# Layer 0 of a two-layer graph network with experts: which queue loads the fixed places, and when the last list writes are issued

## The chip, the cores and the metric

The kernel runs on one core of a Trainium2 chip. The metric is the device time of one execution in microseconds (us), as the median of several runs. Before the change it is 1020.93 us, the median of three runs of 1011.31, 1020.93 and 1027.31 us. A separate execution was taken by the profiler: 1022.18 us, of which 1020.1 us lie between its first and its last instruction (the span). All times in the trace count from the start of that span.

## What is computed

There are 3327 nodes with 256 features each, and a 0/1 adjacency matrix. Two layers follow each other, each with a graph step and a step of routed experts, and each adds its result to its input:

```python
# --- layer 0 (adj_ffn) ---
x = x + _L0_gnn_ref(_layernorm(x, axis=-1), adj, L0_gnn_W, L0_gnn_b)
x = x + _L0_ffn_ref((_layernorm(x, axis=-1))[None], L0_ffn_gate_w, L0_ffn_gate_b, L0_ffn_w1, L0_ffn_w2, L0_ffn_w3)[0]
# --- layer 1 (adj_ffn) ---
x = x + _L1_gnn_ref(_layernorm(x, axis=-1), adj, L1_gnn_W, L1_gnn_a)
...
# _L0_gnn_ref
a = (adj == 1).astype(x.dtype)
deg = jnp.sum(a, axis=1, keepdims=True)
agg = jnp.einsum('ij,jf->if', a, x) / deg
return agg @ W.T + b
...
# _L0_ffn_ref: 16 experts, 256 -> 512 -> 256
probs = jax.nn.softmax(logits, axis=-1)
top_probs, top_idx = jax.lax.top_k(probs, 2)
top_probs = top_probs / jnp.sum(top_probs, axis=-1, keepdims=True)
dispatch = jnp.sum(jax.nn.one_hot(top_idx, n_experts, dtype=x.dtype) * top_probs[..., None], axis=-2)
h1 = jnp.einsum('bsd,edh->bseh', x, w1)
h2 = jnp.einsum('bsd,edh->bseh', x, w2)
hidden = jax.nn.silu(h1) * h2
expert_out = jnp.einsum('bseh,eho->bseo', hidden, w3)
return jnp.einsum('bseo,bse->bso', expert_out, dispatch)
```

The change touches the experts of layer 0 alone.

## The kernel before

Nodes are handled in 26 tiles of 128, taken in chunks of four tiles (the last chunk has two). The graph step of layer 0 (`graph`, line 746) runs over three blocks of chunks: the first three chunks, the fourth, and the last three. For each block it streams the transposed adjacency matrix from memory through SP's queue (`load_adj`, three buffers), DVE turns each piece into a mask (line 698), and TensorE multiplies it with the normalised nodes (line 815). When a block is complete, its chunks go through small closing steps: divide, project, normalise, store the rows in `hd`, compute the gate's logits and route (`dispatch`).

Routing writes a list per expert into `list0` in memory. Each entry is three numbers: where the node's result goes, which row of `hd` to read, and the node's weight. `dispatch` computes each entry's position, and `listed` (line 364) writes 128 entries in one indirect transfer on POOL's queue (line 366). A tile needs two of these, one per chosen expert. For the last block (ten tiles, 20 list writes) the writes are not issued at once: they are put in the list `due` and dealt out later.

The experts of layer 0 then run in slots of up to 256 entries of one expert (`slots0`, line 1095). The first ten slots are fixed: the first 256 entries of experts 0 to 9, all of which come from tiles of the first two blocks. So they start before the last block has been routed. Their entries, the places, are loaded together into the tile `whos` by `routed0` (line 969), which is called before group 21 of the last block's 26 adjacency groups: two transfers on ACT's queue, one for experts 0 and 1 and one for experts 2 to 9. Both depend on the list writes of the first two blocks. Slots from 10 on are chosen by a table and their places are loaded by `places0` on SP's queue; these read lists that must be complete, so they wait for the last list write.

What a slot does, and on which engine:

- `rows_in0` (line 1019): two indirect gathers on POOL's queue bring the slot's rows from `hd` into `xg` (three buffers). They need the slot's places.
- `turned0` (line 1029): TensorE turns the rows (line 1036), half a slot per gather, and ACT copies the result.
- `hidden0` (line 1041), twice, one half of the hidden features each: TensorE (line 1048), then ACT and DVE. The experts' weights come through SP's queue, three transfers of 512 KB per expert (line 998).
- `out0` (line 1066): TensorE (line 1071), DVE scales by the weight (line 1076), and two indirect transfers on POOL's queue add the rows to `xd` in memory (line 1078).

`slots0` yields after each half slot. In the round of slot s it issues the gathers of slot s + 2, turns the rows of slot s + 1, computes the first half of slot s (first yield), closes slot s - 1 with its two adds, and computes the second half of slot s (second yield). `beside` (line 1197) drives it for the first eight slots while the closing steps of the last block are dealt out between, three per half slot. There it also deals out the list writes in `due`. The counter i starts at 1 with the first half of slot 0, so i = 5 and 6 are the halves of slot 2. The deal is three writes per half slot from i = 9 on, the first half of slot 4.

POOL's queue works strictly in the order in which the program issues, and on it lie the list writes, the gathers and the adds. Semaphores that mark transfers as landed are shared in turn: eight for the transfers of SP and ACT together, eight for POOL's. A transfer is issued only when the one that last used its semaphore has landed.

Of the kernel before, what the change touches and what calls it, by code (L numbers as in the profile page):

```python
# [19 lines left out]
P = 128  # L20
# [5 lines left out]
def kernel(  # L26
# [26 lines left out]
    nc = tc.nc  # L53
    N, D = x.shape
    E0, _, H0 = ffn0_w1.shape
    E1, _, H1 = ffn1_w1.shape
# [3 lines left out]
    NP = NT * P  # L60
# [13 lines left out]
    def last_rows():  # L74
# [24 lines left out]
    SA = 2 * P  # L99
    AHEAD_E = 5 * E0 // 8  # L100
# [20 lines left out]
    lists = [  # L121
        dram.tile([E * NP + 2 * P, 3], I32, name=f"list{i}") for i, E in enumerate((E0, E1))
    ]
# [118 lines left out]
    last = {}  # L242
    due = []
# [150 lines left out]
    def rank_table(seen):  # L394

        ps = ps_mm.tile([P, 512], F32, name="mm")
        nc.tensor.matmul(ps[:, :E0], ones_h, seen, start=True, stop=True)

        def small(name, w=E0, dtype=F32):
            return work.tile([P, w], dtype, name=name, bufs=1)  # L400

        key, rank, rest, junk, at = small("k_key"), small("k_rank"), small("k_rest"), small("k_junk"), small("k_at", 2)
        nc.vector.scalar_tensor_tensor(key, ps[:, :E0], float(E0), order_e, op0=OP.mult, op1=OP.add)
        more_ = io.tile([P, 2, D], F32, name="y", bufs=2)[:, 0, : E0 * E0].rearrange("p (a b) -> p a b", b=E0)
        nc.vector.tensor_tensor(more_, key[:, None, :].to_broadcast([P, E0, E0]), key[:, :, None].to_broadcast([P, E0, E0]), op=OP.is_gt)
        nc.vector.tensor_reduce(rank, more_, AX.X, OP.add)
        for i, values in enumerate((rev[:, 0, :], start_e[:, 0, :])):
            nc.vector.scalar_tensor_tensor(junk, rank, slot_p[:, 0:1], values, op0=OP.is_equal, op1=OP.mult, accum_out=at[:, i : i + 1])
        out = small("k_out", 3, I32)
        nc.vector.tensor_scalar(out[:, 0:1], at[:, 0:1], -1.0, float(E0), op0=OP.mult, op1=OP.add)  # L410
        nc.vector.tensor_copy(out[:, 1:2], at[:, 1:2])
        nc.vector.tensor_scalar(out[:, 2:3], at[:, 1:2], float(SA), None, op0=OP.add)
        nc.vector.tensor_scalar(rest, ps[:, :E0], -float(SA), None, op0=OP.add)
        return out, rank, rest
# [132 lines left out]
    def asked(table, s, col=3, name="more"):  # L547

        with in_order(), ExitStack() as behind:
            for name in ("slot", "dve", "act", "pool"):  # L550
                behind.enter_context(tc.issue_after(last[name].ins))
            _, (is_one,) = nc.values_load_multi_w_load_instructions(table[s : s + 1, col : col + 1], min_val=0, max_val=1, bass_reorder=False)
            tc.mark_branch_hint_location(f"{name}{s}", "LikelyTaken", [e.engine for e in (nc.tensor, nc.vector, nc.scalar, nc.gpsimd, nc.sync)])
        return is_one, f"{name}{s}"
# [9 lines left out]
    def in_turn_on_pool():  # L564

        return tc.issue_after(last["pool"].ins) if "pool" in last else nullcontext()
# [383 lines left out]
    early = {}  # L950
# [8 lines left out]
    def places0(s):  # L959

        _, table, row, col, _ = plan[s]
        who = io.tile([P, 2, 3], I32, name="who", bufs=8)
        with in_order():
            at = nc.sync.value_load(early[table][row : row + 1, col : col + 1], min_val=0, max_val=E0 * NP)
        with in_order():
            last["who"] = nc.sync.dma_start(who, lists[0][bass.ds(at, SA), :].rearrange("(h p) w -> p h w", p=P))
        return who

    def routed0():

        with tc.issue_after(last["adj"].ins):
            load0_hidden(0)
        whos = io.tile([P, AHEAD_E, 2, 3], I32, name="whos", bufs=1)
        of = lists[0][: E0 * NP, :].rearrange("(e n) w -> e n w", n=NP)[:, :SA, :].rearrange("e (p h) w -> p e (h w)", p=P)
        for lo, hi in ((0, 2), (2, AHEAD_E)):
            nc.scalar.dma_start(whos[:, lo:hi].rearrange("p e h w -> p e (h w)"), of[:, lo:hi])
        for s in range(AHEAD_E):
            who[s] = whos[:, s]

# [11 lines left out]
    def starts(s):  # L991
        return plan[s][0] != plan[s - 1][0] if s else True

    def next_run(s):
        return next((i for i in range(s + 1, len(plan)) if starts(i)), len(plan))
# [4 lines left out]
    def load0_hidden(s):  # L1000
        run, table, row, _, _ = plan[s]
        if table is None:
            which[run] = slice(run, run + 1)
        else:
            with in_order():
                which[run] = bass.ds(nc.sync.value_load(early[table][row : row + 1, 0:1], min_val=0, max_val=E0 - 1), 1)
        with in_order():
            for i, w in enumerate((ffn0_w1, ffn0_w2)):
                load0(s, i, w[which[run]].rearrange("o (p k) h -> p (o k) h", k=KD))

    def load0_out(s):
        with in_order():
            load0(s, 2, ffn0_w3[which.pop(plan[s][0])].rearrange("o (a p b) d -> p (o a) b d", p=P, b=2))
# [5 lines left out]
    def rows_in0(s):  # L1019
        xg = io.tile([P, 2, D], F32, name="xg", bufs=3)  # L1020
        for h, m in parts0(s):
            with in_turn_on_pool():
                last["pool"] = nc.gpsimd.indirect_dma_start(  # L1023
                    out=xg[:m, h, :], out_offset=None, in_=hd_of[0][: NE0 * P, :] if s < AHEAD_E else hd[:, :],
                    in_offset=bass.IndirectOffsetOnAxis(ap=who[s][:m, h, 1:2], axis=0),
                )
        return xg
# [67 lines left out]
    def slots0(first, end):  # L1095
        usual = not first
        for s in range(first - 3, end + 1):
            if usual and s in AHEAD_AT:
                graph1_ahead(AHEAD_AT.index(s))
            if usual and s == AHEAD_E - 2:  # L1100
                early["rank"], *early["ranks"] = rank_table(seen0)
            if usual and s == AHEAD_E + 2:
                early["spill"] = spill_table(*early["ranks"], seen_head)
            if usual and s == end - 2:
                early["more"] = asked(early["spill"], 0)
            if s == first - 1 and first:
                load0_hidden(first)
            if first <= s < end and starts(s):
                if next_run(s) < end:
                    load0_hidden(next_run(s))  # L1110
                load0_out(s)
            known = AHEAD_E if s < AHEAD_E - 2 else end
            for i in range(max(who, default=-1) + 1, min(s + 4, known)):
                who[i] = places0(i)
            for i in range(max(xg, default=-1) + 1, min(s + 3, known)):
                xg[i] = rows_in0(i)
            if first <= s + 1 < end:
                xT[s + 1] = turned0(s + 1, xg[s + 1])
            if first <= s < end:
                hid[s] = [hidden0(s, xT[s], 0)]  # L1120
                if usual:
                    head1(2 * (s - LATE0))
                yield
            if first <= s - 1:
                out0(s - 1, hid.pop(s - 1))
            if first <= s < end:
                hid[s].append(hidden0(s, xT.pop(s), 1))
                if usual and s == end - 1:
                    spare = const.tile([P, 1], F32, name="spare")
                    nc.scalar.activation(spare, half[:, 0:1], AF.Exp, bias=hid[s][1][:, 0, 0:1], scale=0.0)  # L1130
                if usual:
                    head1(2 * (s - LATE0) + 1)
                yield
            elif s == first - 1:
                yield


# [49 lines left out]
    def graph1_ahead(i):  # L1187
        with in_order():
            a = load_adj(pools1[1], GRAPH[0], groups_of(GRAPH[0])[i])
        if i < AHEAD:  # L1190
            ahead1[1][0, i] = mask_of(a, pools1[2], GRAPH[0], groups_of(GRAPH[0])[i], 0.0, OP.not_equal)
        else:
            ahead1[0][0, i] = a

    slots = slots0(0, USUAL0)

    def beside(post):

        for i, _ in enumerate(slots, 1):
            for _ in range(3):  # L1200
                next(post, None)
            for _ in range(3 if i > 8 else 0):
                if due:
                    due.pop(0)()
            if i == 2 * (AHEAD_E - 2):
                break
        assert not due and next(post, None) is None
# [200 lines left out]
```

## Time and profile before

| What | Value |
|---|---|
| Median of three runs | 1020.93 us (1011.31 to 1027.31) |
| Profiled execution | 1022.18 us |
| Its span | 1020.1 us |
| Mean granted TensorE clock | 0.961 |
| Busy time of DVE, ACT, POOL | 493.1, 257.6, 429.7 us |
| Issue of the two places' transfers on ACT | 200.2 and 200.7 us |
| First gather of slot 0 | 202.94 us |
| First and last list write of the last block | 277.93 and 322.29 us |
| Mean of one list write on POOL (line 366) | 1057 ns, 104 of them |
| Median of one gather of the fixed slots (line 1023) | 977 ns, 20 of them |
| Mean of one add of the fixed slots (line 1078) | 1619 ns, 20 of them |

How to read it: an engine's busy time counts its instructions alone; a wait is put down to the event that came last before the instruction could start. The time of a transfer on POOL's queue in the timeline is the time in which POOL builds it; the data land later, and that is given as the time from issue to landing. In lines of the timeline the columns are start, length, engine, line of the kernel, operation, what is written and read, how many were merged, and in brackets the idle time before and what ended it. Tables of stretches give, for each stretch, its length, the busy time of PE, PEld (weight load of TensorE), DVE, ACT and POOL, the granted clock, the DMA engines' busy share and GB/s.

### The profile page before, as it was taken

Reading aid. Unit: us, or ns where it says so; the run is one execution under the profiler, and the core shown is the slowest. Engines: PE = TensorE matmul, PEld = TensorE weight load, DVE = VectorE, ACT = ScalarE, POOL = GpSimd, SP = SyncE. Lnnn points to the kernel's source line nnn. Section 1 sums busy time; section 2 is a strip of 40 time slices with the busy share of each in tenths; the row PEclk is TensorE's granted clock in tenths of the full one; section 3 lists DMA queues with packets and bytes.
Section 4 is the critical chain, followed back from the end, with each engine's and each line's share of the span. In section 5 each row is a group of like instructions: output and inputs, shape, how many; then the busy total and the mean of one; then the engine's idle time right before and its main releaser. Section 6 shows DMA issues by size and latency. Waiting matters only on the chain. (4 is left out here: it accounts for less than half of the span.)

```text
span 1020.1 us, 14285 instructions
## 1 busy us (share of the span) xinstructions
PE 931.9 (91%) x4505; PEld 783.9 (77%) x4505; DVE 493.1 (48%) x1797; ACT 257.6 (25%) x530; POOL 429.7 (42%) x407
## 2 busy tenths in 40 slices
PE   7899999899997999999999999999889578999991
PEld 5677887688886999888987777877667357888880
DVE  7565585254622322212123577667576541343764
ACT  3310311024311111111111444130222323444440
POOL 2040062522476454454453311005251475777762
PEclk9999999898998999999999999999899789999996
DMA  9988677856677656677888398868954865333376
GB/s 335 326 299 285 230 181 234 236 176 200 183 160 165 192 161 149 162 207 211 225 262 251 76 312 285 254 211 188 253 110 150 256 180 166 95 94 93 93 260 209
DMA packets 109328, 207.00 MB, mean 203 GB/s; under 512 B 30595, under 2 KB 63044, under 8 KB 109246
## 3 DMA queue, kind: packets, MB, share of 16 engines
q1 hardware_dynamic: 68384, 157.30, 49.3%
q0 software_dynamic: 20528, 30.56, 13.3%
q10 hardware_dynamic: 20334, 18.17, 6.1%
q8 instruction: 36, 0.59, 0.3%
q14 instruction: 46, 0.38, 0.2%
HBM read 176.82 MB, written 35.47 MB: 208 GB/s over the span
## 5 line engine op out<-in xcount | busy, mean ns | idle before, releaser
L815 PE MATMUL acc<-big,y 128*128 128x512 f32 (+2 forms) x1456 | 344.9, 391 | 25.4 <-DVE big L698 15.0
L815 PEld LDWEIGHTS acc<-big,y 128*128 128x128 f32 (+1 forms) x1456 | 265.0, 194 | 82.0 <-ACT y L871 9.0
L1048 PE MATMUL acc<-xT,w 128*128 128x256 f32 (+3 forms) x1024 | 213.3, 362 | 0.0
L1048 PEld LDWEIGHTS acc<-xT,w 128*128 128x128 f32 x1024 | 186.0, 200 | 16.5 <-issue 3.5
L366 POOL DMA_INDIRECT list<-where,t_idx x104 | 109.9, 1057 | 187.3 <-DVE t_idx L361 63.1
L698 DVE TENSOR_SCALAR big<-adj 128x1536 fp32r<-128x1536 int32 (+6 forms) x130 | 111.7, 864 | 118.0 <-DMA adj<-in_adj_t 79.9
L1071 PE MATMUL acc<-w,hid 128*128 128x256 f32 (+3 forms) x512 | 118.0, 381 | 0.0
L1056 DVE TENSOR_TENSOR hid<-hid,acc 128x512 f32<-128x512 f32 (+3 forms) x64 | 40.0, 624 | 145.3 <-PE acc L1048 138.3
L1078 POOL DMA_INDIRECT xd<-y,who x44 | 67.7, 1539 | 100.0 <-DVE y L1076 64.0
L1071 PEld LDWEIGHTS acc<-w,hid 128*128 128x128 f32 (+3 forms) x512 | 89.1, 178 | 20.1 <-issue 3.6
L1052 ACT ACTIVATE hid<-acc 128x512 f32<-128x512 f32 (+3 forms) x64 | 35.0, 547 | 212.7 <-PE acc L1048 200.1
L620 POOL DMA_INDIRECT zd<-y,who x58 | 70.6, 1218 | 29.2 <-DVE y L1291 16.1
L1277 ACT ACTIVATE h<-acc,v 128x256 f32<-128x256 f32 x116 | 54.9, 474 | 102.8 <-PE acc L1274 101.8
L1274 PE MATMUL acc<-xT,v 128*128 128x256 f32 x232 | 63.6, 398 | 6.1 <-DMA v<-w1d 5.5
L595 POOL DMA_INDIRECT xg<-hd,who x58 | 57.2, 986 | 26.4 <-issue 21.3
L1274 PE MATMUL acc<-h,v 128*128 128x256 f32 x232 | 61.1, 387 | 0.6 <-ACT h L1277 0.6
L1289 DVE TENSOR_TENSOR y<-acc,v 128x512 f32<-128x512 f32 x29 | 20.0, 691 | 81.5 <-PE acc L1286 81.5
L270 POOL TENSOR_TENSOR ln_var<-ln_var,half 128x2 f32<-128x2 f32 (+2 forms) x19 | 15.2, 802 | 102.5 <-DVE ln_var L268 80.6
L1078 POOL DMA_INDIRECT xd<-y,whos x20 | 32.4, 1619 | 60.5 <-DVE y L1076 42.5
L1286 PE MATMUL acc<-v,h 128*128 128x256 f32 x232 | 56.7, 387 | 0.1
L1274 PEld LDWEIGHTS acc<-xT,v 128*128 128x128 f32 x232 | 44.6, 203 | 14.8 <-issue 5.3
L1023 POOL DMA_INDIRECT xg<-hd,who x44 | 43.0, 977 | 18.8 <-issue 11.0
(282 smaller groups left out, 970.7 us busy)
## 6 DMA issues: line engine op xcount, KB each, us to landing
adj<-in_adj_t SPq DMA_DIRECT2D x66, 768.0 KB, 6.3
w<-in_ffn_w SPq DMA_DIRECT2D x78, 512.0 KB, 5.8
adj<-in_adj_t SPq DMA_DIRECT2D x25, 639.5 KB, 6.7
adj<-in_adj_t SPq DMA_DIRECT2D x25, 512.0 KB, 4.6
v<-w1d SPq DMA_DIRECT2D x7, 898.0 KB, 9.3
hd<-ln_h ACTq DMA_DIRECT2D x12, 512.0 KB, 10.7
w_all<-w1d SPq DMA_DIRECT2D x6, 898.0 KB, 15.6
w1d<-in_ffn_w ACTq DMA_DIRECT2D x18, 256.0 KB, 5.3
```

Of the source, the lines that this page charges most:

```text
L366: ins = nc.gpsimd.indirect_dma_start(out=rows_of[2 * (t0 + j) + i], out_offset=bass.IndirectOffsetOnAxis(ap=idx[:, i, j : j + 1], axis=0), ...
L595: last["pool"] = nc.gpsimd.indirect_dma_start(out=xg[:, h, :], out_offset=None, in_=of, in_offset=bass.IndirectOffsetOnAxis(ap=who[:, h, 1 ...
L620: last["z"] = nc.gpsimd.indirect_dma_start(out=zviews[n * s + h], out_offset=bass.IndirectOffsetOnAxis(ap=who[:, h, 0:1], axis=0), in_=y[: ...
L698: last["mask"] = nc.vector.tensor_scalar(mask[:kr, :, :cols], a[:kr, :, :cols], value, None, op0=op)
L815: last["graph"] = nc.tensor.matmul(acc[c][k][:, :w], y[:kr, j, part, k * P : (k + 1) * P], mask[:kr, jj, i0 : i0 + w], start=(j == 0 and p ...
L1023: last["pool"] = nc.gpsimd.indirect_dma_start(out=xg[:m, h, :], out_offset=None, in_=hd_of[0][: NE0 * P, :] if s < AHEAD_E else hd[:, :], ...
L1048: last["slot"] = nc.tensor.matmul(q[:, c, :n], w[:, k, h0 : h0 + 2 * P - 1 : 2], xT[:, k, :n], start=(k == 0), stop=(k == KD - 1))
L1071: nc.tensor.matmul(ps[:m, h, :], hid[c // 2][:, c % 2, h * P : h * P + m], w3[:, c // 2, c % 2, :], start=(c == 0), stop=(c == NC0 - 1))
L1078: ins = last["pool"] = nc.gpsimd.indirect_dma_start(out=xd_of[2 + h] if s < USUAL0 else xd, out_offset=bass.IndirectOffsetOnAxis(ap=who[s] ...
L1274: ins = nc.tensor.matmul(ps[:, c, :], w[:, k, c : H1 : NC1], src[:, k, :], start=(k == 0), stop=(k == 1))
L1277: last["act"] = nc.scalar.activation(dst[:, c, :], ps[:, c, :], AF.Relu, bias=w1s[s % 3][:, BB + 2 * i + c : BB + 2 * i + c + 1])
L1286: nc.tensor.matmul(ps[:, h, :], h2[:, c, h * P : (h + 1) * P], w[:, c, :], start=(c == 0), stop=(c == NC1 - 1))
```

## The change

The places of the fixed slots are loaded on POOL's queue instead of ACT's. The first transfer (experts 0 and 1) stands where both stood before; the second (experts 2 to 9) is issued from `slots0` at s = -1, behind the gathers of slots 0 and 1. Both are kept in turn with POOL's other indirect work.

The 20 list writes of the last block are dealt from i = 6 on, the second half of slot 2: 5, 3, 4, 3, 3 and 2 at i = 6 to 11.

```diff
+    def fixed_places(lo, hi):
+
+        of = lists[0][: E0 * NP, :].rearrange("(e n) w -> e n w", n=NP)[:, :SA, :].rearrange("e (p h) w -> p e (h w)", p=P)
+        with in_turn_on_pool():
+            last["pool"] = nc.gpsimd.dma_start(early["whos"][:, lo:hi].rearrange("p e h w -> p e (h w)"), of[:, lo:hi])
+
     def routed0():
 
         with tc.issue_after(last["adj"].ins):
             load0_hidden(0)
         whos = io.tile([P, AHEAD_E, 2, 3], I32, name="whos", bufs=1)
-        of = lists[0][: E0 * NP, :].rearrange("(e n) w -> e n w", n=NP)[:, :SA, :].rearrange("e (p h) w -> p e (h w)", p=P)
-        for lo, hi in ((0, 2), (2, AHEAD_E)):
-            nc.scalar.dma_start(whos[:, lo:hi].rearrange("p e h w -> p e (h w)"), of[:, lo:hi])
+        early["whos"] = whos
+        fixed_places(0, 2)
         for s in range(AHEAD_E):
             who[s] = whos[:, s]
...
             elif s == first - 1:
+                if usual:
+                    fixed_places(2, AHEAD_E)
                 yield
...
+    DEALT = {6: 5, 7: 3, 8: 4, 9: 3, 10: 3, 11: 2}
+
     def beside(post):
 
         for i, _ in enumerate(slots, 1):
             for _ in range(3):
                 next(post, None)
-            for _ in range(3 if i > 8 else 0):
-                if due:
-                    due.pop(0)()
+            for _ in range(DEALT.get(i, 0)):
+                due.pop(0)()
             if i == 2 * (AHEAD_E - 2):
                 break
```

## The prediction

> **What bounds the kernel now.** I read the page first, then the waits of TensorE in the stretch that the diff touches, then that stretch on TensorE and on POOL in order of time, and last SP's queue.
>
> ```profile
> PE 931.9 (91%) x4505; PEld 783.9 (77%) x4505; DVE 493.1 (48%) x1797; ACT 257.6 (25%) x530; POOL 429.7 (42%) x407
> ```
>
> TensorE is busy 91% of the 1020.1 us span; a change that adds no matmul can win only at its gaps. The diff acts between about 200 us (the places are loaded) and 323 us (the last list write). TensorE's waits from 196 to 345 us (total, times, longest):
>
> ```profile
> PE acc L1036 <- DMA xg<-hd,whos: 7.4, 3, 4.5
> PE acc L815 <- DVE big L700: 4.4, 1, 4.4
> PE mm L1036 <- DMA xg<-hd,whos: 1.1, 1, 1.1
> ```
>
> L1036 turns a slot's gathered rows. So 8.5 us go to gathers that land late. The 4.4 us (194 to 198 us) end with a mask whose adjacency load was issued at 184.37 us, before anything changed; it stays. TensorE in order of time (start, length, idle before):
>
> ```profile
> 297.87 0.51 PE L1036 MATMUL acc<-ident,xg 128*128 128x128 f32 x2 [1.64 <-DMA xg<-hd,whos]
> ...
> 319.41 0.17 PE L397 MATMUL mm<-seen,ones_h 128*128 128x16 bf16 x1
> 324.13 0.67 PE L1036 MATMUL acc<-ident,xg 128*128 128x128 f32 x2 [4.54 <-DMA xg<-hd,whos]
> 326.06 0.70 PE L1036 MATMUL acc<-ident,xg 128*128 128x128 f32 x2 [1.25 <-DMA xg<-hd,whos]
> 326.55 5.31 PE L1048 MATMUL acc<-xT,w 128*128 128x256 f32 x16
> ```
>
> Slot 7 (slots counted from 0) costs 12.74 us from hidden layer to hidden layer (285.47 to 298.21) where the undisturbed step is 10.83 (298.21 to 309.04): 1.91 lost. Slot 9 starts at 326.55 where 309.04 + 10.83 = 319.87 would do: 6.68 lost. Its first 16 matmuls take 5.31 us instead of 3.63, another 1.68: the granted clock was 0.50 from 324 to 328 us. Together **10.27 us**, all that the new dealing can win. After 327 us TensorE has no gap until 552 us, so what is won or lost here moves the rest of the layer.
>
> POOL in the same stretch shows why the gathers are late:
>
> ```profile
> 260.34 1.57 POOL L1078 DMA_INDIRECT xd<-y,whos  x1 [0.30 <-DVE rden L761]
> 262.21 1.00 POOL L1023 DMA_INDIRECT xg<-hd,whos  x1 [0.30 <-issue]
> 263.52 0.97 POOL L1023 DMA_INDIRECT xg<-hd,whos  x1 [0.30 <-issue]
> 271.53 1.62 POOL L1078 DMA_INDIRECT xd<-y,whos  x1 [7.04 <-DVE y L1076]
> ...
> 277.93 1.00 POOL L366 DMA_INDIRECT list<-where,t_idx  x1 [0.30 <-issue]
> ...
> 318.41 0.99 POOL L1023 DMA_INDIRECT xg<-hd,whos  x1 [0.30 <-issue]
> ```
>
> From 282.5 to 327 us POOL never rests. A slot costs it two adds (3.77 us with their gaps), two gathers (2.60) and six list writes (7.75): 14.1 us against TensorE's 10.8 per slot. It falls behind until the lists are through; but it stood idle 7.04 us before 271.53.
>
> SP's queue between 196 and 210 us has one wait that belongs to the places:
>
> ```profile
> SPq L687 <- DMA whos<-list: 10.7, 1, 10.7
> ```
>
> An adjacency load is ready to go once its buffer is read (mask done 198.06) but is issued at 202.19, just after the first places land (200.24 plus 1.9). In the order of the built instructions it waits for a hardware-queue semaphore that the first places' transfer holds; in the changed kernel it no longer does. In that time the DMA engines stood nearly still (last two columns: share, GB/s):
>
> ```profile
> 198.00:200.00 2.00, 1.89 (x5) 1.52 (x6) 0.90 (x4) 0.00 (x0) 0.00 (x0) 0.50 0.32 93
> 200.00:202.00 2.00, 2.00 (x7) 1.63 (x6) 0.83 (x1) 0.00 (x0) 0.00 (x0) 0.50 0.12 10
> ```
>
> **The change, part 1: the dealing.** The built order on PE, DVE and SP is the same; POOL's becomes, from slot 1's adds: 5 lists, gathers 5, 3 lists, adds 2, 4 lists, gathers 6, 3 lists, adds 3, 3 lists, gathers 7, 2 lists, adds 4, gathers 8. The first 16 lists have their indices at 259.0 us and the other four at 277.6, before POOL comes to them, so no new wait stands in the queue. With a list at 1.295 us, POOL runs:
>
> - adds 1 end 261.91; 5 lists from 262.21 to 268.7; gathers 5 at 268.7 and 270.0 (6.5 us later than now).
> - 3 lists to 275.2; adds 2 to 278.9 (their rows are ready at 271.6); 4 lists to 284.1; **gathers 6 at 284.1 and 285.4**, 8.8 us later than now.
> - 3 lists to 290.6; adds 3 to 294.4; 3 lists to 298.25; gathers 7 at 298.25 and 299.55; 2 lists to 303.4, the last list 19 us earlier than now; adds 4, gathers 8 at 307.2; no list afterwards.
>
> TensorE wants gathers 5 at 274.0, 6 at 285.0, 7 at 295.8. Landing after issue took 2.7 to 3.2 us with the DMA engines quiet (slot 3) and 5.3 to 7.2 while weights were moving. Gathers 5 go out when the share was 0.65, then 0.01 (268 to 272 us): with 2.9 to 4 us they land by 274, no wait; with 6.3 at 276.3, 2 us. Gathers 6 go out 0.6 us after a 512 KB weight load (283.5) and just ahead of two more (285.2). That is the position of slot 9's gathers today (318.41, after a weight load at 317.9), which landed in 5.6 and 6.3 us. So they land at 289.7 and 291.7: TensorE waits 4.7 us, turns half the slot, waits 1.7 more. It is slot 9's stall over again (4.54 and 1.25), clock included (1.7): 6.4 + 1.7 + 0.3 for slow turns = 8.4. A wait at slot 5 would not add to it, since the end is set by POOL's 285.4. With quiet engines the stall is 3.0 and the clock stays up; that is one end. At the other, gathers 7 land 6.4 us after 299.55, at 306.0 against a wish of 296.2: 9.8 in all. I hold them at no wait: TensorE, 8.4 us late, asks at 304.3, and between its weight loads (285.2, next 302.7) the engines are quiet, as for slot 8 today (2.9 to 3.9 us). Slots 8 and 9 find POOL without lists. Sum of part 1: 8.4 instead of 10.27, **-1.9 us**, between -7.3 and -0.5.
>
> The earlier end of the lists is worth nothing by itself: slot 10's places now wait for it (landed 329.0) and TensorE still finds slot 10's rows in time at 338.6.
>
> **Part 2: the places on POOL.** Two ACT issues (0.38 and 0.48 us) go; ACT had nothing else to do until 212.0. POOL gets two, in one place each: before slot 0's gathers, and between slot 1's and slot 2's. Behind the first wait all eight gathers, and behind slot 0's gathers TensorE, which turns its second half at 211.49 after 1.06 us of waiting. Issue cannot come before the lists land (200.1). POOL's plain transfers took 0.54 to 1.06 us; this one moves 256 runs of 24 bytes, nearest to an indirect one of 128 rows, 0.97. Its landing: 1.9 us on ACT with idle engines is one end, 6.6 (the last list writes, under load) the other. Since SP's adjacency load now goes at 198.1, the engines are busy, and I take 4. Slot 0's gathers then go at 204.7 and 206.0 instead of 202.94 and 204.25. But SP's 2.8 MB (two adjacency blocks, three weights) go 4.1 us earlier too, and are through by about 210 instead of 214: I take 6 us for the second gather, 212.0, **+0.5 us**; ends -1.1 (the wait disappears) and +4.5 (6.6, then 7.2).
>
> The Trainium skill speaks against this part (DMA: Bandwidth & Descriptors, Issuing engine by pattern): a plain load belongs on a hardware queue, GpSimd is for the indirect ones, and its specification table has about 1 us to the first byte for GpSimd's path against 0.6. By that alone the estimate for part 2 would be +0.4, with nothing gained; the same page (Issuing engines are not separate DMA queues) would save an issuing engine's time and no more, where the row above shows 4.1 us for which SP's load stood.
>
> The second places' transfer (1024 runs) has until about 219 to be issued and landed: slot 2's gathers need some 10 us before TensorE turns them at 229.1. By the gather's rate (0.97 us for 128 rows) it takes at most 7.8 us from about 209, and some 3 to 6 to land; I put it at no cost, 4 us at worst. Slot 3 is asked for only at 245.8.
>
> Sum: -1.9 + 0.5 = -1.4. The profiled execution took 1022.18 us (span 1020.1 and 2.1 around it) and would take 1020.8; it was 1.25 above the median of the three, so I predict 1020.93 - 1.4 = **1019.5**.
>
> **Rivals.** *The stall goes altogether* (0.15): if DMA is quiet at 284 us, or POOL gets through the lists faster than 1.295 each, slots 6 and 7 cost 0 to 3 us: 1020.9 - 10.3 to -7.3, near 1012. For it: the 7.04 us of POOL's idle time are really used. Against: gathers 6 are issued 0.9 us before they are wanted, and no gather landed in under 2.7. *The places are slow on POOL* (0.2), the slower side: the 1024 short runs hold POOL or land late, slot 2's gathers follow, and from a landing past 219 us each us is paid by TensorE; at 12 us over the point that is +12, less 2 from the dealing, and slow clock after so long a gap: about 1032. Against it: the 7.8 us bound. *It does nothing at all* (0.1): the places land as before and the stall only changes its slots, gathers 7 being late too; 1020.93 - 0.5 = 1020.4. My forecast has 0.55.
>
> **The numbers.** Main case with its ends: 1020.93 - 8.4 to + 4 gives 1012.5 to 1025. With the rivals, and with three runs that spread from 1011.3 to 1027.3, I take **1009 to 1030**. Two per cent, about what this kernel's scatter lets a measurement tell from no change, is 20.4 us, beyond every worked sum: faster 0.06, within 0.84, slower 0.10, the slow places having the only open end.
>
> **What would show it.** Right: TensorE's waits at L1036 have one gap of 4 to 5 us near 285 and none at 298 or 319 to 326; clock 0.5 there; last list near 302; no SP wait on the places; DMA share above 0.5 in 198 to 202. Wrong: no gap near 285 (then nearer 1012), or a gap at 229 (the places), or TensorE's first turn well past 212.

## The result, and the profile after

| Kernel | Median | Lowest to highest | Ratio to before, 95% interval |
|---|---|---|---|
| before | 1017.68 us (20 runs) | 1006.22 to 1030.09 | 1 |
| after | 1023.09 us (20 runs) | 1017.29 to 1030.21 | 1.008 [1.0056, 1.0104] |

The change makes the kernel 0.8% slower (5.7 to 10.6 us by the interval), where the forecast had 1.4 us less; the medians of all runs differ by 5.4 us. (Ratios leave disturbed executions out, so here and below they need not be the ratio of the medians: the ratio of e14_places_again below rests on four of its eleven runs, and the traces of e5, e8 and e14 are of executions that were left out.) The profiled execution of after took 1021.68 us, with a span of 1019.2 us and a clock of 0.956. The profiled one of before took 1022.18 us, 4.5 us over the median of its own 20 runs, so the two spans say nothing on the change. Single stretches have to be compared.

The busy times, from the page of after: no matmul has been added, but 4.7 us more of TensorE time; the mean granted clock is 0.956 for 0.961.

```profile
PE 936.6 (92%) x4505; PEld 784.0 (77%) x4505; DVE 496.2 (49%) x1797; ACT 257.5 (25%) x530; POOL 432.4 (42%) x409
```

TensorE's waits for gathered rows in after, 196 to 345 us (total, times, longest):

```profile
PE acc L1041 <- DMA xg<-hd,whos: 6.6, 2, 4.4
PE mm L1041 <- DMA xg<-hd,whos: 4.3, 2, 3.9
PE mm L1041 <- DMA xg<-hd,who: 3.6, 2, 2.2
```

Line 1041 is the turning (1036 before). The first row is a stall at slot 6. It replaces the 7.4 us in three waits at slots 7 and 9. The second is slot 0: 4.3 us for 1.1. The third was not there before: it names `who`, not `whos`, so it is a slot behind the fixed ones. TensorE of after in order of time (start, length, engine and line, what, idle before):

```profile
288.98 0.67 PE L1041 MATMUL acc<-ident,xg 128*128 128x128 f32 x2 [4.36 <-DMA xg<-hd,whos]
291.89 0.70 PE L1041 MATMUL acc<-ident,xg 128*128 128x128 f32 x2 [2.24 <-DMA xg<-hd,whos]
...
325.84 0.17 PE L397 MATMUL mm<-seen,ones_h 128*128 128x16 bf16 x1
325.87 0.72 PE L1041 MATMUL acc<-ident,xg 128*128 128x128 f32 x4
326.43 3.63 PE L1053 MATMUL acc<-xT,w 128*128 128x256 f32 x16
...
339.13 0.51 PE L1041 MATMUL mm<-ident,xg 128*128 128x128 f32 x2 [2.17 <-DMA xg<-hd,who]
341.05 0.70 PE L1041 MATMUL mm<-ident,xg 128*128 128x128 f32 x2 [1.41 <-DMA xg<-hd,who]
```

Slot 6 stalls as forecast (4.7 and 1.7 us were said). Slots 7, 8 and 9 do not wait, and slot 9's hidden layer starts at 326.43 at full clock. Then slot 10 waits, 2.17 and 1.41 us. POOL in the same stretch:

```profile
283.56 0.99 POOL L1028 DMA_INDIRECT xg<-hd,whos  x1 [0.31 <-issue]
284.85 0.97 POOL L1028 DMA_INDIRECT xg<-hd,whos  x1 [0.30 <-issue]
...
335.32 1.01 POOL L1028 DMA_INDIRECT xg<-hd,who  x1 [7.41 <-PE acc L1053]
336.63 0.97 POOL L1028 DMA_INDIRECT xg<-hd,who  x1 [0.30 <-issue]
```

Gathers 6 go out at 283.56 and 284.85 (284.1 and 285.4 were worked out). But before slot 10's gathers POOL stands idle for 7.41 us: the lists have long been written, and it waits for slot 10's places. Those are loaded at 329.84 by SP, which must first read the rank table, which DVE ends at 328.63, from the matmul at line 397 at 325.84 (DVE and SP of after):

```profile
328.49 0.14 DVE L412 TENSOR_SCALAR k_out<-k_at 128x1 int32<-128x1 f32 x1
329.84 1.59 SPq L966 DMA_DIRECT2D who<-list  x2
```

The bracket of the first gather names TensorE, whose semaphore moved last; but the trace has the last update of the places' own semaphore at 334.50, and the gather starts 0.82 us later. In before it also starts 0.82 us after the places have landed (331.87 and 332.69), and there the bracket names the places. From the matmul at line 397 to the second turn of slot 10 it takes 15.2 us. TensorE has 10.9 us of work to put against it (slot 9's turns and matmuls).

At the places, POOL of after, and then stretches of 2 us (length, PE, PEld, DVE, ACT, POOL, clock, DMA share, GB/s):

```profile
197.97 0.78 POOL L973 DMA_DIRECT2D whos<-list  x1 [4.79 <-DMA list<-where,t_idx]
205.04 1.00 POOL L1028 DMA_INDIRECT xg<-hd,whos  x1 [6.28 <-DMA whos<-list]
206.34 0.95 POOL L1028 DMA_INDIRECT xg<-hd,whos  x1 [0.30 <-issue]
```

```profile
198.00:200.00 2.00, 2.00 (x12) 1.73 (x11) 0.07 (x2) 0.00 (x0) 0.75 (x1) 1.00 0.99 358
200.00:202.00 2.00, 2.00 (x12) 1.73 (x11) 0.83 (x2) 0.00 (x0) 0.00 (x0) 1.00 1.00 251
```

The first gather starts 7.07 us after the places' issue (2.70 before): SP no longer waits for the places, its adjacency block moves at once, and the DMA engines are full (0.99 and 1.00, where they were at 0.32 and 0.12) while the places land. But the rows then come quickly, and what follows on TensorE is this:

```profile
207.97 0.67 PE L1041 MATMUL mm<-ident,xg 128*128 128x128 f32 x2 [3.86 <-DMA xg<-hd,whos]
209.06 0.70 PE L1041 MATMUL mm<-ident,xg 128*128 128x128 f32 x2 [0.42 <-DMA xg<-hd,whos]
209.41 4.37 PE L815 MATMUL acc<-big,y 127*128 127x512 f32 x12
```

TensorE of before at the same place:

```profile
211.49 0.51 PE L1036 MATMUL mm<-ident,xg 128*128 128x128 f32 x2 [1.06 <-DMA xg<-hd,whos]
211.75 2.56 PE L815 MATMUL acc<-big,y 127*128 127x512 f32 x12
```

From the places' issue to slot 0's second turn it is 197.97 to 209.06 = 11.09 us, against 200.24 to 211.49 = 11.25: the rows are as early as before. New is that TensorE, whose masks come sooner, has nothing to do ahead of them for 3.86 us, and that the last twelve mask matmuls then take 4.37 us instead of 2.56 (the granted clock was 0.50 from 208 to 212 us, 1.00 in before from 210 to 214). From the issue to the end of the masks: 15.81 us against 14.07, 1.7 us lost.

### The profile page after: what moved, and what is told of

The parts are those of the page before. It is cut to its first block, busy times and chain, and to the rows that moved or that the text cites. A ratio compares the mean times of both kernels' runs of the same rounds, so it can differ in the third digit from the quotient of the medians.

```text
span 1019.2 us, 14286 instructions
## 1 busy us (share of the span) xinstructions
PE 936.6 (92%) x4505; PEld 784.0 (77%) x4505; DVE 496.2 (49%) x1797; ACT 257.5 (25%) x530; POOL 432.4 (42%) x409
## 5 line engine op out<-in xcount | busy, mean ns | idle before, releaser
L1053 PE MATMUL acc<-xT,w 128*128 128x256 f32 (+3 forms) x1024 | 215.5, 364 | 0.0
L595 POOL DMA_INDIRECT xg<-hd,who x58 | 67.3, 1161 | 25.3 <-issue 15.2
L620 POOL DMA_INDIRECT zd<-y,who x58 | 61.6, 1062 | 28.1 <-DVE y L1299 12.3
L1028 POOL DMA_INDIRECT xg<-hd,who x44 | 42.9, 976 | 20.5 <-issue 11.6
## 6 DMA issues: line engine op xcount, KB each, us to landing
w_all<-w1d SPq DMA_DIRECT2D x6, 898.0 KB, 11.3
```

Source lines behind the costliest of these rows:

```text
L595: last["pool"] = nc.gpsimd.indirect_dma_start(out=xg[:, h, :], out_offset=None, in_=of, in_offset=bass.IndirectOffsetOnAxis(ap=who[:, h, 1 ...
L620: last["z"] = nc.gpsimd.indirect_dma_start(out=zviews[n * s + h], out_offset=bass.IndirectOffsetOnAxis(ap=who[:, h, 0:1], axis=0), in_=y[: ...
L1028: last["pool"] = nc.gpsimd.indirect_dma_start(out=xg[:m, h, :], out_offset=None, in_=hd_of[0][: NE0 * P, :] if s < AHEAD_E else hd[:, :], ...
L1053: last["slot"] = nc.tensor.matmul(q[:, c, :n], w[:, k, h0 : h0 + 2 * P - 1 : 2], xT[:, k, :n], start=(k == 0), stop=(k == KD - 1))
```

## The experiments

The four sets were run on three chips. The kernel before took 1049 and 1056 us in the first two (one chip), 1020 us in each of the last two, like the first comparison. Beside the time the table gives two durations from each trace, both from the first turn of a slot: slot 1 to slot 12, and slot 9 to slot 12 (three undisturbed slots: 32.5 us). "Late" is the rank table, which chooses the slots from 10 on, where it was, "early" a slot sooner. "Even" is explained with the second set.

| Run | Places | Dealing | Table | Median (us) | Ratio [95%] | 1 to 12 (us) | 9 to 12 (us) |
|---|---|---|---|---|---|---|---|
| before | ACT | old | late | 1017.68 | 1 | 145.69 | 36.15 |
| after | POOL | new | late | 1023.09 | 1.008 [1.0056, 1.0104] | 151.12 | 39.30 |
| e1_deal_only | ACT | new | late | 1050.31 | 1.0005 [0.9969, 1.0042] | 150.10 | 38.06 |
| e2_places_only | POOL | old | late | 1052.82 | 1.0045 [1.0014, 1.0076] | 152.06 | 45.65 |
| e3_table_early | POOL | new | early | 1048.72 | 1.0014 [0.9978, 1.005] | 143.82 | 32.51 |
| e4_places_on_sp | SP | old | late | 1050.50 | 1.0043 [1.0015, 1.0071] | 144.71 | 38.99 |
| e5_after_again | POOL | new | late | 1061.01 | 1.0015 [0.9979, 1.0052] | 154.15 | 40.14 |
| e6_before_again | ACT | old | late | 1051.98 | one run | 146.91 | 36.91 |
| e7_deal_table | ACT | new | early | 1047.32 | 0.9946 [0.9914, 0.9979] | 145.47 | 32.50 |
| e8_even_table | ACT | even | early | 1049.36 | 0.9929 [0.9898, 0.9959] | 147.27 | 32.51 |
| e9_table_only | ACT | old | early | 1014.65 | 0.9923 [0.9885, 0.996] | 139.24 | 33.38 |
| e10_even_pool | POOL | even | early | 1015.70 | 0.9951 [0.9914, 0.9988] | 136.98 | 32.51 |
| e11_even_again | ACT | even | early | 1014.49 | 0.9919 [0.9879, 0.9958] | 138.56 | 32.51 |
| e12_even_split | both | even | early | 1017.27 | 0.9985 [0.9951, 1.0018] | 136.27 | 32.50 |
| e13_deal_again | ACT | new | late | 1025.14 | 1.0035 [0.9995, 1.0074] | 151.73 | 38.19 |
| e14_places_again | POOL | old | late | 1027.48 | 0.9987 [0.9937, 1.0036] | 151.56 | 42.21 |
| e15_table_again | POOL | new | early | 1020.62 | 1.0016 [0.998, 1.0051] | 144.13 | 32.51 |
| e16_even_only | ACT | even | late | 1018.99 | 1.0007 [0.997, 1.0044] | 145.60 | 38.26 |

### First set: each half alone, the table earlier, the places on SP

The dealing alone is the diff's second part on the kernel before; the places alone are its first part. The early table, on the changed kernel:

```diff
-            if usual and s == AHEAD_E - 2:
+            if usual and s == AHEAD_E - 3:
                 early["rank"], *early["ranks"] = rank_table(seen0)
...
-            known = AHEAD_E if s < AHEAD_E - 2 else end
+            known = AHEAD_E if s < AHEAD_E - 3 else end
```

The places on SP's queue, on the kernel before:

```diff
+    def places_fixed():
...
-            nc.scalar.dma_start(whos[:, lo:hi].rearrange("p e h w -> p e (h w)"), of[:, lo:hi])
+            with tc.issue_after(last["adj"].ins):
+                last["who"] = nc.sync.dma_start(whos[:, lo:hi].rearrange("p e h w -> p e (h w)"), of[:, lo:hi])
```

> The new dealing alone; the places stay on ACT's queue. Theory A (the dealing only moves the loss: slot 9's stall used to cover the chain rank table, places, gathers of slot 10): TensorE waits about 4 and 2 us for slot 6's gathers near 290 us, has no wait at slots 7 and 9, and waits 3 to 4 us for slot 10's gathers near 340 us, with the clock near 0.5 after both; time +2 to +6 us over the kernel before. Rival B (the whole loss comes from the places): no wait at slot 10 beyond 1 us and time -3 to 0 us. Rival C (the loss lies in layer 1 or is chance): time within 2 us and the waits as in A.

> The places on POOL's queue, the old dealing. Theory A: the first places land 5 to 7 us after their issue on POOL where ACT's took 1.9, TensorE waits 3 to 5 us before it turns slot 0 and runs at a clock near 0.5 after it; slots 7 and 9 stall as in the kernel before, slot 10 does not; time +1 to +4 us. Rival B (the whole loss comes from the places): +5 to +8 us. Rival D (freeing SP's queue pays for it): -3 to +1 us.

> The changed kernel with the rank table and slot 10's places one slot earlier. Theory A: slot 10's gathers are issued right behind slot 6's adds, the wait near 340 us and its slow clock go, and the time is 5 to 7 us below the changed kernel, so -2 to +2 us against the kernel before. Rival B: the wait at slot 10 goes but the time stays at +4 to +8 us, since something later is late anyway.

> The kernel before with the places on SP's queue, behind the last full adjacency load, so that no adjacency load is held by them. Theory A (what counts is how soon the first places land, not SP's hold): issue near 200 us, landing in 2 to 4 us, TensorE waits at most 2 us before slot 0, rest as before; time -2 to +1 us. Rival D (SP's hold cost 4 us): -5 to -3 us.

On this chip no time but those of the places alone and of the places on SP leaves 1, and those by 0.4%. The early table brings the changed kernel no time here: 1.0014, and 1.0015 without it (e5_after_again, next set), where theory A had 5 to 7 us. The waits say more. The early table does away with slot 10's wait: 32.51 us from slot 9 to slot 12. The dealing alone has that wait (1.01 and 2.24 us) and so have the places alone (4.41 and 3.12), although their dealing is the old one. That speaks against both theories in their simple form: slot 10's wait is not the dealing's own. The stall expected at slot 6 of the dealing alone is not in its trace. On SP, behind the adjacency block, the first gather starts 5.34 us after the places' issue, TensorE waits 1.6 us at slot 0 as theory A had it, and the time is 0.4% over before, which neither theory had.

This chip also has stalls that the others do not show. In e3_table_early, ScalarE:

```profile
276.18 1.28 ACT L1057 ACT_TABLE_LOAD   x1
283.12 0.60 ACT L1057 ACTIVATE hid<-acc 128x512 f32<-128x512 f32 x1 [5.65 <-remote]
```

"remote" is a release that belongs to no instruction and no transfer in the trace. TensorE stands still for 7.14 us there. No trace of the first comparison or of the last two sets has one. In layer 0 they fall on slots 4 to 8 and hide or add to the stalls in question, which is why whole times on this chip separate the theories badly.

### Second set: after and before on that chip, and two better versions

Early table with places on ACT and the changed dealing; then also an even dealing:

```diff
-    DEALT = {6: 5, 7: 3, 8: 4, 9: 3, 10: 3, 11: 2}
+    DEALT = {6: 3, 7: 2, 8: 3, 9: 2, 10: 3, 11: 2, 12: 3, 13: 2}
```

> The changed kernel itself, measured beside the others of this set on one chip. Theory A (two places in layer 0 pay: slot 0's rows come 2 to 4 us late because the places land late on GpSimd's queue, and slot 10's rows come 3 to 4 us late because nothing covers the chain from the rank table to the gathers): ratio 1.004 to 1.009, TensorE waits of 2 to 4 us in front of slot 0's turns and of 2 to 5 us in all in front of slot 10's. Theory B (the places alone pay): the same ratio, but the waits at slot 10 are no longer than those of the kernel before on this chip. Theory C (layer 0 has nothing to do with it, the first comparison was chance): ratio 0.997 to 1.003.

> The kernel before, for its trace on the same chip as the others of this set. Theory A: SP's second load of a late adjacency group held some 10 us by the fixed slots' places, slot 0's rows at most 1.5 us late, a stall at slot 9 (or, where slot 9 is in time, one at slot 10 of the size that the changed kernel shows). Theory B: as A, but slot 10's waits as long as the changed kernel's. Theory C: no prediction for single waits; a time as the kernel before beside it.

> The places on ScalarE's queue as before, the changed dealing, and the rank table and slot 10's places and rows a slot earlier. Theory A: no late places at slot 0 beyond before's 1 us, waits at slot 6 of 4 to 7 us (the dealing still puts four and five list writes in front of the gathers of slots 5 and 6), none at slots 9 and 10: against before 0.994 to 0.999. Theory B: as the kernel before or as the dealing alone, 0.997 to 1.003, the table's place without effect. Theory C: 0.997 to 1.003 and waits without any relation to the dealing.

> As the kernel before it in this set, but the twenty writes dealt 3, 2, 3, 2, 3, 2, 3, 2 from the third slot on. Theory A: GpSimd falls behind by 1 to 2 us a slot at most, so no wait over 2 us at slots 5 to 9 and none at slot 10: against before 0.989 to 0.996, the lowest of this set. Theory B: as the kernel before, 0.997 to 1.003. Rival within A (the stall goes nowhere but to the next slot whatever the dealing, since GpSimd's work of layer 0's beginning is all on the path): waits at slots 7 to 9 that sum to 4 to 8 us, ratio 0.997 to 1.002.

In the traces of after and before the waits are as theory A had them: in after waits of 2.06 and 0.53 us at slot 0, and of 2.29 and 1.98 at slot 10; in before a stall at slot 9 (5.23 and 2.01), 1.66 us at slot 8 and none at slot 10. The time of after does not leave 1 here (1.0015, where theory A had 1.004 to 1.009). Both versions with the early table are faster than before, by 0.5 and 0.7%, as theory A had it; their traces are not what it had. The waits expected at slot 6 of e7_deal_table are missing, and in e8_even_table, where none over 2 us was expected at slots 5 to 9, TensorE stands still for 6.26 and 1.74 us at slot 8. Extra stalls of this chip lie close by in both. Whether the table or the dealing makes the gain was open.

### Third set: the table alone, and the places' queue with all else equal

```diff
+        of = lists[0][: E0 * NP, :].rearrange("(e n) w -> e n w", n=NP)[:, :SA, :].rearrange("e (p h) w -> p e (h w)", p=P)
+        nc.scalar.dma_start(whos[:, :2].rearrange("p e h w -> p e (h w)"), of[:, :2])
-        fixed_places(0, 2)
```

is the edit of e12_even_split on e10_even_pool; e9_table_only is before with the two lines of the table alone.

> The kernel before with nothing changed but the rank table and slot 10's places and rows a slot earlier. Theory A (slot 10's chain counts only where the lists end early and no stall at slots 6 to 9 covers it): the lists of the old dealing still end too late for slot 10's places to leave earlier, and slot 9's stall stays: ratio 0.996 to 1.002, TensorE waits at slot 9 (or 8) of 4 to 8 us as in the kernel before. Rival (the table's place alone gains, the dealing nothing): 0.991 to 0.996, as the earlier kernels with an early table.

> The changed kernel's places on GpSimd's queue, with the dealing 3, 2, 3, 2, 3, 2, 3, 2 and the early table. It differs from the third kernel of this set in the queue of the places alone. Theory A (the places on GpSimd's queue let the first gathers start 6.4 to 7.7 us after their issue, on ScalarE's 2.5 to 2.7): first gathers 6 to 8 us after the issue, TensorE waits 2 to 4 us in front of slot 0's turns, time 0.2 to 0.6% over the third kernel. Theory C (no cost there, since SP's load of the late adjacency is freed in exchange): within 0.2% of the third kernel.

> The places on ScalarE's queue, the dealing 3, 2, 3, 2, 3, 2, 3, 2 and the early table, a second time, as the mark for the other three. Theory A: 0.990 to 0.996 of the kernel before, as the first time (0.9929). Theory C: 0.997 to 1.003, the first time by chance.

> As the second kernel of this set, but the places of the first two experts on ScalarE's queue, those of the next eight on GpSimd's behind the gathers of slots 0 and 1. Theory A (only the first transfer's way to its landing costs): first gathers 2.5 to 3 us after the issue, no wait over 1.5 us at slot 0, time within 0.2% of the third kernel or below it. Rival within A (the second transfer on GpSimd's queue costs as much, by holding the gathers of slot 2): gathers of slot 2 at the same distance after those of slot 1 as in the changed kernel, 2 to 3 us, and a wait in front of slot 2's turns of 1 us or more, time as the second kernel.

The rival won in the first of them: the table's place alone gives 0.9923, as much as table and even dealing together (0.9919). So my theory that slot 10's chain counts only where the lists end early was wrong. The trace of before, in which slot 9's stall lies in front of that chain and covers it, is one case; places alone and places on SP, both with the old dealing, show the other. With the old dealing the stalls at slots 7 to 9 differ from trace to trace: 7.4 us in before, 8.9 in e6_before_again, 3.2 in e9_table_only, 3.1 in e14_places_again. So a part of what the trace of e9_table_only gains is that its slot 9 does not stall, and why it does not is not shown. In e9_table_only slot 10's places are also loaded ahead of the last two list writes, which wait for them on POOL (3.07 us), so there the chain is rid of the lists as well as of the table.

The queue of the places is 0.3% apart (0.9951 and 0.9919) with intervals that overlap: not settled by the time. The first gathers started 7.9 us after the issue on POOL and 2.5 on ACT, as expected. The split version, expected at most 0.2% over places on ACT, came out at 0.9985: 0.7% over it (the intervals just touch), and no faster than before in spite of the early table, though its trace has the shortest stretch from slot 1 to slot 12 of all. What costs it that time is not shown. In it the first gathers started 3.1 us after the issue, and still TensorE waited at slot 0 (POOL, then TensorE, of e12_even_split):

```profile
203.20 1.00 POOL L1029 DMA_INDIRECT xg<-hd,whos  x1 [8.67 <-issue]
204.50 0.97 POOL L1029 DMA_INDIRECT xg<-hd,whos  x1 [0.30 <-issue]
```

```profile
210.81 1.24 PE L1042 MATMUL mm<-ident,xg 128*128 128x128 f32 x4 [2.87 <-DMA xg<-hd,whos]
```

So neither theory had slot 0 right: the queue moves the first gather and not the rows. The traces of the last two sets (by their numbers) and of the first comparison, from the places' issue on:

| Places | Traces | Issue to second turn of slot 0 | Last twelve mask matmuls | Issue to end of the masks |
|---|---|---|---|---|
| ACT | before, e9, e11, e13, e16 | 11.2 to 11.3 us | 2.56 to 2.58 us | 14.0 to 14.1 us |
| POOL | after, e10, e14, e15 | 11.1 to 12.0 us | 4.00 to 4.62 us | 15.8 to 17.0 us |
| split | e12 | 11.3 us | 3.90 us | 15.5 us |

The rows land within a microsecond of each other whatever the queue. With ACT, SP's block is held: it is issued 1.7 to 2.0 us after the places in all five ACT traces, and 2.9 to 4.0 us ahead of them in the POOL and split ones. So with ACT the masks come later, and TensorE works on them while the rows are under way; without the hold it is through with them, stands idle for 2.9 to 3.9 us in one piece, and does the rest at a lower clock. From the last list write's start to the issue it is 4.5 to 6.7 us in the ACT rows and 6.9 to 7.3 in e10, e14 and e15, so a little more may be lost ahead of the issue.

### Fourth set: the halves again, on a chip without the extra stalls

> The dealing alone (places on ScalarE's queue, table at its old place). Theory A (the dealing gains 1 to 2 us up to slot 9 and pays 5 to 7 at slot 10, the places pay 1 to 4 at slot 0): waits at slot 6 of 4 to 7 us, at slot 10 of 3 to 5 us and a slow clock behind them; ratio 1.002 to 1.006. Theory B (the places pay for it all): 0.997 to 1.001.

> The places on GpSimd's queue alone (old dealing, table at its old place). Theory A: first gathers 6.4 to 7.7 us after the issue, 2 to 4 us of waits in front of slot 0's turns, the wait at slots 7 to 9 as in the kernel before; ratio 1.001 to 1.005. Theory B: 1.005 to 1.009, the whole loss of the changed kernel.

> The changed kernel with the rank table and slot 10's places and rows a slot earlier. Theory A: no wait over 1 us at slot 10, and so 0.4 to 0.7% under the changed kernel: ratio 1.000 to 1.004 where the changed kernel gave 1.008. Theory B: as the changed kernel, 1.005 to 1.009.

> The dealing 3, 2, 3, 2, 3, 2, 3, 2 from the third slot on, places on ScalarE's queue, table at its old place. If the table's place made the gain of the earlier versions: waits at slot 10 of 2 to 5 us, ratio 0.998 to 1.003. If the dealing's shape made it: no wait over 1 us at slot 10 and at most 3 us in all at slots 6 to 9, ratio 0.990 to 0.996.

TensorE of e13_deal_again, e14_places_again, e15_table_again and e11_even_again, each at slot 10 (and, in the third, line 397):

```profile
339.00 0.50 PE L1036 MATMUL mm<-ident,xg 128*128 128x128 f32 x2 [2.06 <-DMA xg<-hd,who]
340.96 0.70 PE L1036 MATMUL mm<-ident,xg 128*128 128x128 f32 x2 [1.46 <-DMA xg<-hd,who]
```

```profile
344.89 0.50 PE L1041 MATMUL mm<-ident,xg 128*128 128x128 f32 x2 [4.45 <-DMA xg<-hd,who]
347.82 0.70 PE L1041 MATMUL mm<-ident,xg 128*128 128x128 f32 x2 [2.44 <-DMA xg<-hd,who]
```

```profile
320.30 0.17 PE L397 MATMUL mm<-seen,ones_h 128*128 128x16 bf16 x1
320.32 0.72 PE L1041 MATMUL acc<-ident,xg 128*128 128x128 f32 x4
...
331.25 0.63 PE L1041 MATMUL acc<-ident,xg 128*128 128x128 f32 x4
331.72 3.63 PE L1053 MATMUL acc<-xT,w 128*128 128x256 f32 x16
```

```profile
333.10 0.63 PE L1036 MATMUL mm<-ident,xg 128*128 128x128 f32 x4
333.57 0.60 PE L1048 MATMUL acc<-xT,w 128*128 128x256 f32 x2
```

The dealing alone repeats after's slot 10 to about 0.1 us, and the places alone have the stall at slot 10 too, larger, since in that execution slot 8 stalled and slot 9 did not. Each half alone loses from slot 1 to slot 12 about what both together lose, 5.4 to 6.0 us (151.73, 151.56 and 151.12, against 145.69). With the table a slot earlier (third fence, line 397 in front of slot 8's turns) slot 9's turns and, in the fourth fence, slot 10's follow without a wait. The changed kernel with the early table runs at 1.0016 [0.998, 1.0051], where the changed kernel gave 1.008 [1.0056, 1.0104]: most of the loss is gone, though the two were not measured beside each other. The even dealing alone gains nothing (1.0007): slot 10 waits 2.04 and 1.58 us. The halves' own times (1.0035 and 0.9987, each with 0.4 to 0.5% to either side) are too wide to share the loss between them.

## Why the prediction was wrong

**Slot 6 and POOL's order: right.** Gathers 6 came within 0.6 us of the worked times, waits of 4.36 and 2.24 us stood for 4.7 and 1.7, the clock was 0.50 from 290 to 294 us, slots 7 to 9 did not wait, the last list was built by 302.57 (303.4 was said). All the signs that were named for being right came; none of them lay behind 326 us, where the loss turned up. From slot 1's first turn to the end of slot 9's first 16 matmuls: 116.01 us in after, 117.27 in before. The dealing is 1.3 us ahead there; the forecast had 1.9. (In e13_deal_again, the dealing alone, the same stretch took 117.73 us, so it is not shown that the dealing gains there.)

**The step that failed: "The earlier end of the lists is worth nothing by itself: slot 10's places now wait for it (landed 329.0) and TensorE still finds slot 10's rows in time at 338.6."** In before, slot 10's places waited for two things, the last lists and the rank table, and both were covered because slot 9 had just stalled: the table's matmul stood at 319.41, ahead of that stall, and its chain had 19.2 us until 338.6. POOL and TensorE of before at slot 10:

```profile
332.69 1.01 POOL L1023 DMA_INDIRECT xg<-hd,who  x1 [5.66 <-DMA who<-list]
338.60 0.63 PE L1036 MATMUL mm<-ident,xg 128*128 128x128 f32 x4
```

I took slot 10's punctuality for a property of slot 10. It was paid for by slot 9's stall. With that stall gone, the chain from line 397 (15.2 us to the second turn) meets one slot of work (10.9 us). From slot 9's first turn to slot 12's it costs 39.30 - 32.51 = 6.8 us in after, where the same stretch of before holds 3.6 us, the rest of slot 9's own stall. The 1.3 us turned into a loss of 5.4 us from slot 1 to slot 12 (that the medians differ by 5.4 too is chance, as the sum below shows). The early table shows the cause of the wait: with it the stretch is 32.5 us in seven of eight traces (33.38 in the one with the old dealing), and each of the eight traces with the late table and no stall over 1 us at slot 9 has waits of 3.2 to 7.5 us at slot 10. In these eight SP issues the places 1.2 to 1.3 us after DVE has ended the table, so the table sets their time; in before and e6_before_again it is 6.9 and 7.5 us, since the last lists end later there. In time the table gains 0.6 to 0.9% over the same kernel without it in four of five pairs (after, the dealing alone, the even dealing, before); two of these pairs were not measured beside each other, and the changed kernel on the chip of the first two sets gained nothing.

**Part 2: the wrong term.** The +0.5 was a difference in when slot 0's second rows land (212.0 for 211.49). The first gather came later than I had it, 7.07 us after the issue for 4.6, the landing of the rows was shorter, 2.7 us for 6, and the sum came out at -0.2. The cost lies where I counted nothing: freeing SP's load (forecast rightly: no wait on the places, DMA share 0.99 and 1.00 from 198 to 202 us) brings the masks forward, out of the time in which they had covered the rows' flight, and the idle time slows the clock for the masks that are left: +1.7 us. The second places' transfer cost nothing visible; no wait stood at slot 2.

With 5.4 from slot 1 on it makes 7.1 us in these two traces. They are not the whole account, for from slot 12 to its end the trace of after is 5.8 us shorter than that of before. Most of that is in layer 1, where TensorE waits for the experts' weights (800 to 900 us; before, then after):

```profile
PE acc L1274 <- DMA v<-w1d: 5.5, 2, 5.0
PE acc L1282 <- DMA v<-w1d: 0.5, 1, 0.5
```

This goes with the places' queue: the wait is 3.8 to 5.5 us in the five ACT traces of the table above and 0.5 to 3.0 in the POOL and split ones, and from layer 1's first matmul with these weights to the end it takes 200.1 to 201.5 us in the former and 196.8 to 198.1 in the latter. So the places on POOL give back some 3 us late in the kernel, which the prediction did not have either; why is not shown. By the traces some 4 us of loss would be left, where the medians say 5.4 and the ratio 5.7 to 10.6 (0.56 to 1.04% of 1017.68). Each part rests on single traces, and the times of the halves did not settle their shares.

The Trainium skill's rule in DMA: Bandwidth & Descriptors, Issuing engine by pattern, puts plain loads on a hardware queue. The first gather did start later with the places on POOL (6.4 to 7.9 us after the issue, 2.5 to 2.7 on ACT with a quiet DMA, 5.3 on SP), far more than the 0.4 us between that page's first-byte latencies; the rows, which are what TensorE waits for, were at 11.1 to 12.0 us against 11.2 to 11.3.

**The rivals.** The slower side was put at the places' second transfer holding slot 2. It did not. That a stall would turn up beyond the fixed slots was in no rival, though the line 397 row stood in the prediction's own fence.

## What to carry to other kernels

A stall covers whatever chain runs beside it, so before removing one, list every chain that starts ahead of it and is wanted after it, and measure each against the work that is left without the stall (here 15.2 us against 10.9); in the same way a freed wait moves work, and that work may have been the cover of something else, as the masks were for slot 0's rows. Where such a chain hangs on a table that could be computed sooner, move the table: these two lines made the kernel 0.8% faster than before (0.9923 [0.9885, 0.996]), which no dealing alone did. With the places on ACT and the even dealing the early table beat the kernel before twice (0.9929 and 0.9919), so it is a version to take further; that the even dealing adds anything to the two lines is not shown.

## What the runs showed of the hardware that was not expected

The clock fell after less idle time than I had thought. In e11_even_again two waits of 0.60 and 1.42 us in front of slot 8 were followed by 4 us at a clock of 0.57 (columns as above):

```profile
308.00:310.00 2.00, 0.58 (x3) 0.39 (x4) 1.93 (x15) 0.00 (x0) 1.70 (x2) 1.00 0.99 353
310.00:312.00 2.00, 2.00 (x7) 1.65 (x8) 1.69 (x10) 0.59 (x1) 1.70 (x2) 0.57 1.03 313
312.00:314.00 2.00, 2.00 (x7) 1.62 (x6) 0.14 (x1) 0.21 (x1) 1.47 (x2) 0.57 0.85 123
```

In before, one wait of 1.64 us at slot 7 left it at 1.00. The Trainium skill (TensorE: Matmul & The Clock Gate, What's actually happening) puts the drop after an idle window of about 3.4 us; here two waits of 2.0 us in all, 0.5 us of turning between them, were enough, so short waits that follow each other closely must be counted with the clock. And on one of the three chips of the experiments the kernel before took 3% longer (1049 and 1056 us against 1020), and its traces alone have stalls, of up to 10 us, that end with no recorded release; that these make the 3% was not tried.
